# A transformer layer with two kinds of attention: the causal part's order, later features, and the last norm's root on ScalarE

## The chip, the cores and the metric

The kernel runs on one core of a Trainium2 chip. The metric is the device time of one execution in microseconds (us), the median of several runs; lower is better. Times within the kernel come from a profile of one execution. The engines are TensorE (PE, with its weight loads PEld), VectorE (DVE), ScalarE (ACT), GpSimd (POOL) and SyncE (SP), which here only issues DMAs.

## What is computed

A layer in three parts, each with a layer norm before and a residual after. All numbers are float32. `x` is 4 x 256 x 256 (batch, token, channel), the context 4 x 4096 x 256, with 16 heads of 16 channels.

```python
x = x + cross_attention(layernorm(x), ctx, ctx)     # softmax over 4096 context rows
x = x + causal_attention(layernorm(x))              # positive features, no softmax
x = x + ffn(layernorm(x))                           # silu(x Wg) * (x Wu), then Wd; hidden 768

# causal_attention, for each batch and head:
qf, kf = features(q), features(k)   # exp(clip(omega . x/|x| * sqrt(2 s) - s)), 64 features
ctx[t] = sum_{u <= t} (qf[t] . kf[u]) v[u]
den[t] = max(sum_{u <= t} qf[t] . kf[u], 1e-6)
out = (ctx / den) @ Wout + bout
```

## The kernel before

The first 1063 us are the cross attention; the change touches what follows, the **causal part** and the feed-forward part that is woven into it (lines 374 to 594 of the kernel).

Work is cut by batch `b` (4, of 256 tokens, two row tiles of 128) and by quad `q` (4 heads). A step `n` from 0 to 15 is one quad of one batch, `n = 4 b + q`. `attend(n)` (line 413) makes three functions of a step.

- `scores` (420): on TensorE the products of key and query features, into four PSUM banks `pa` (lines 427 and 432). Two of them are copied to `at` by ScalarE (438) and masked by GpSimd (439); the other two are masked by VectorE on the way out (444).
- `values` (447): `at` times V, the sums of four heads in one bank `po` (453); ScalarE copies it to `avT` (458). V has a column of ones, so the denominators come along.
- `divide` (461), once for two quads: transposes `avT` into `pt_o` on TensorE (465), then three VectorE instructions: the clamp and reciprocal of `den` (470, 471) and the product into `att` (472).

`features(n)` (273) makes the features of quads `n` and `n + 1` in one go: eight products into four banks `pf` (281), four clips on VectorE (287), four exponentials on ScalarE (288), four factors on GpSimd (289). Those of the first six quads are made during the cross attention.

`output(b)` (479) transposes `att` of a batch (`tr_o`, 486), copies it on ScalarE (`oT`, 487), multiplies by Wout (`py`, 492) and adds to the residual stream `xr` (493). `feed_forward(b)` (495) makes four functions: `norm` (layer norm, on VectorE), `turn` (transposes `tr_z`, 509, copied to `zT` by ScalarE, 510), `hidden(m)` for three pairs of 128 columns (`pg` and `pu`, 518; tanh on ScalarE, 522; two VectorE instructions into `hT`, 523 and 524) and `down(i)` for the two row tiles (`pd`, twelve products in all, 530; the sum, 534; the store, 535).

There are two layer norms in the code. `layernorm` (96) takes the root with ScalarE's Sqrt (109) and a reciprocal on VectorE. `normalised` (137), used in this part, finds the inverse root on VectorE alone with `inverse_root` (120): two instructions for a first guess and three for each of three refinements.

What sets the order: TensorE, ScalarE, VectorE and SyncE run their instructions in the order in which the program writes them (`manual_schedule`, line 539); GpSimd's order is left to the framework. A loop over `n` from 0 to 16 (584) writes, for each step, the values of the step before, the scores of this one, the divide when `n` is even, a features call for the steps in `early`, and then what the list `fills[n]` holds. All PSUM tiles come from one pool of eight banks.

The `fills` hold the pieces of other work. `weight(n)` (402) turns a piece of the integer feed-forward weights, which `weight_load` (395) brings by DMA on SyncE's queue, into floats on ScalarE, and starts the load after next. `normalise`, `turn15` and `project15` (819, 845, 853) end the cross attention: `normalise` transposes the last sums (`pt_x`), divides them on VectorE (`rd`, `on`), adds a bias on GpSimd (836) and sends them with eight DMAs on SyncE's queue into rows (`xo`, 840); `turn15` transposes those rows (`px`, 849) and `project15` multiplies them by Wh (`py` at line 159) and adds to `xr` (858). Until then the norm of the last batch (`norm3`) can't start, nor its `turn3` (`tr`, 208, copied to `zT` by VectorE, 209), its queries and keys (`qk3`, products `pqk`, sum at 221) and values (`v3`). `normed`, `qk_normed` (259) and `qk_turned` (264, 265) turn them into the input of features 12 and 14.

For batch `b`, output and norm stand in step `4b + 4`, the turn in the step behind it, hidden and down in the steps from there on. For the last batch everything is in step 16, with what is left of the batch before it.

Of the kernel before, what the change touches and what calls it, by code (L numbers as in the profile page):

```python
# [12 lines left out]
F32 = mybir.dt.float32  # L13
I32 = mybir.dt.int32
AF = mybir.ActivationFunctionType
# [5 lines left out]
P = 128  # L21
B, T, D = 4, 256, 256
# [12 lines left out]
NH = HID // P  # L35
# [4 lines left out]
def perceiver_layer(  # L40
# [5 lines left out]
    nc = tc.nc  # L46
# [17 lines left out]
    eps = const.tile([P, 1], F32, tag="eps", name="eps")  # L64
# [31 lines left out]
    def layernorm(z, tiles):  # L96

        n = len(tiles)
        mv = lnp.tile([P, n, 2], F32, tag="ln_mv", name="ln_mv")
        rs = lnp.tile([P, n], F32, tag="ln_rs", name="ln_rs")  # L100

        def stats():
            for i, t in enumerate(tiles):
                st = lnp.tile([P, 6], F32, tag="ln_st", name="ln_st")
                nc.vector.bn_stats(st, xr[:, t, :])
                nc.vector.bn_aggr(mv[:, i, :], st)

        def root():
            nc.scalar.activation(rs, mv[:, :, 1], AF.Sqrt, bias=eps)

        def scaled():
            nc.vector.reciprocal(rs, rs)
            for i, t in enumerate(tiles):
                nc.vector.tensor_scalar(
                    z(t), xr[:, t, :], mv[:, i, 0:1], rs[:, i : i + 1], ALU.subtract, ALU.mult
                )

        return stats, root, scaled
# [18 lines left out]
    def normalised(z, tiles):  # L137

        n = len(tiles)
        mv = lnp.tile([P, n, 2], F32, tag="ln_mv", name="ln_mv")  # L140
        for i, t in enumerate(tiles):
            st = lnp.tile([P, 6], F32, tag="ln_st", name="ln_st")
            nc.vector.bn_stats(st, xr[:, t, :])
            nc.vector.bn_aggr(mv[:, i, :], st)
        v = lnp.tile([P, n], F32, tag="ln_v", name="ln_v")
        nc.vector.tensor_scalar(v, mv[:, :, 1], LN_EPS, None, ALU.add)
        rs, pieces = inverse_root(v)
        for piece in pieces:
            piece()
        for i, t in enumerate(tiles):  # L150
            nc.vector.tensor_scalar(
                z(t), xr[:, t, :], mv[:, i, 0:1], rs[:, i : i + 1], ALU.subtract, ALU.mult
            )
# [31 lines left out]
    def bank(shape, name):  # L185

        return psum.tile(shape, F32, tag="b", name=name)
# [187 lines left out]
    late = ctx.enter_context(tc.tile_pool(name="late", bufs=1))  # L375
# [4 lines left out]
    for i in (0, 2):  # L380
# [2 lines left out]
            pattern=[[1, P]], channel_multiplier=-1,  # L383
        )
    att = late.tile([P, NT, D], F32, tag="att", name="att")

# [13 lines left out]
    def weight(n):  # L402
        i, half = divmod(n, 2)
        w = ws[i].shape[1] // 2
        nc.scalar.activation(
            ws[i][:, half * w : half * w + w, :], coming.pop(n), AF.Copy, scale=(1.0, 0.5, 1.0)[i] / 127.0
        )
        if n + 2 < 6:
            weight_load(n + 2)
# [69 lines left out]
    def output(b):  # L479
        tiles = (2 * b, 2 * b + 1)  # L480
        oTs = []
        for t in tiles:
            oT = work.tile([P, KC, P], F32, tag="oT", name="oT")
            ps = bank([P, KC, P], "tr_o")
            for k in range(KC):
                nc.tensor.transpose(ps[:, k, :], att[:, t, k * P : (k + 1) * P], ident)
            nc.scalar.copy(oT, ps)
            oTs.append(oT)
        for t, oT in zip(tiles, oTs):
            py = bank([P, D], "py")  # L490
            for k in range(KC):
                nc.tensor.matmul(py, lhsT=oT[:, k, :], rhs=wout_sb[:, k, :], start=k == 0, stop=k == KC - 1)  # L492
            nc.vector.tensor_tensor(xr[:, t, :], py, xr[:, t, :], ALU.add)

    def feed_forward(b):

        tiles = (2 * b, 2 * b + 1)
        z = work.tile([P, 2, D], F32, tag="z", name="z")
        zT = work.tile([P, KC, T], F32, tag="zT", name="zT")
        hT = work.tile([P, NH, T], F32, tag="hT", name="hT")  # L500

        def norm():
            normalised(lambda t: z[:, t % 2, :], tiles)

        def turn():
            ps = bank([P, KC, 2, P], "tr_z")
            for j in range(2):
                for k in range(KC):
                    nc.tensor.transpose(ps[:, k, j, :], z[:, j, k * P : (k + 1) * P], ident)
            nc.scalar.copy(zT.rearrange("p k (j t) -> p k j t", t=P), ps)  # L510

        def hidden(m):
            pg, pu = bank([P, 2, T], "pg"), bank([P, 2, T], "pu")
            for ps, w in ((pg, wg), (pu, wu)):
                for i in range(2):
                    ns = slice((2 * m + i) * P, (2 * m + i + 1) * P)
                    for k in range(KC):
                        nc.tensor.matmul(  # L518
                            ps[:, i, :], lhsT=w[:, k, ns], rhs=zT[:, k, :], start=k == 0, stop=k == KC - 1
                        )  # L520
            th = work.tile([P, 2, T], F32, tag="th", name="th")
            nc.scalar.activation(th, pg, AF.Tanh, scale=0.5)
            nc.vector.scalar_tensor_tensor(th, th, 1.0, pg, ALU.add, ALU.mult)
            nc.vector.tensor_tensor(hT[:, 2 * m : 2 * m + 2, :], pu, th, ALU.mult)

        def down(i):
            t = tiles[i]
            pd = bank([P, D], "pd")
            for n in range(NH):
                nc.tensor.matmul(  # L530
                    pd, lhsT=hT[:, n, i * P : (i + 1) * P], rhs=wd[:, n, :], start=n == 0, stop=n == NH - 1
                )
            o = work.tile([P, D], F32, tag="o", name="o")
            nc.vector.tensor_tensor(o, pd, xr[:, t, :], ALU.add)
            nc.sync.dma_start(out=out[t * P : (t + 1) * P, :], in_=o)

        return norm, turn, hidden, down

    with tc.manual_schedule(engines={ET.PE, ET.Activation, ET.DVE, ET.SP}):
        normalise, turn15, project15 = finish  # L540
        normalise()
        for n in range(2):
            weight_load(n)
        NB = B * NQ
        fills = {n: [] for n in range(NB + 1)}
        norm3, turn3, qk3, sq3, v3, _ = causal_in(3)
        for n in range(6):
            fills[n + 1] += [lambda n=n: weight(n)]
        fills[2] += [turn15]
        fills[3] += [project15, norm3]  # L550
        fills[4] += [turn3, lambda: qk3(0)]
        fills[5] += [lambda: qk3(1), lambda: sq3(0), v3, lambda: sq3(1), lambda: normed((6, 7))]
        fills[6] += [lambda: qk_normed(6), lambda: qk_normed(7)]
        fills[7] += [lambda: qk_turned(6), lambda: qk_turned(7)]
        ff = {}

        def call(b, part, *args):
            return lambda: ff[b][part](*args)

        def begin(b):  # L560
            ff[b] = feed_forward(b)
            ff[b][0]()

        for b in range(B):
            n0 = 4 * b + 4
            turn, down = call(b, 1), [call(b, 3, i) for i in range(2)]
            hidden = [call(b, 2, m) for m in range(NH // 2)]
            fills[n0] += [lambda b=b: output(b), lambda b=b: begin(b)]
            if b < B - 1:
                fills[n0 + 1] += [turn]  # L570
                fills[n0 + 2] += [hidden[0]]
            if b < B - 2:
                fills[n0 + 3] += [hidden[1]]
                fills[n0 + 4] += [hidden[2]]
                fills[n0 + 5] += down
            elif b == B - 2:
                fills[n0 + 3] += [hidden[1]]
                ends = [hidden[2]] + down
            else:
                fills[n0][:0] = ends[:1]  # L580
                fills[n0] += ends[1:] + [turn] + hidden + down
        early = {0: 6, 2: 8, 4: 10, 8: 12, 10: 14}
        steps = [attend(n) for n in range(NB)]
        for n in range(NB + 1):
            if n > 0:
                steps[n - 1][1]()
            if n < NB:
                steps[n][0]()
            if n > 0 and n % 2 == 0:
                steps[n - 1][2]()  # L590
            if n in early:
                features(early[n])
            for piece in fills[n]:
                piece()
# [503 lines left out]
```

## Time and profile before

| | us |
|---|---|
| median of 3 runs | 1214.21 (1213.54 to 1215.38) |
| the profiled execution | 1214.88 |
| its span in the profile | 1213.2 |
| end of the cross attention's last products | 1063.1 |
| PE busy | 1183.5 (98%) |
| DVE busy | 905.8 (75%) |
| ACT busy | 686.8 (57%) |
| POOL busy | 142.3 (12%) |
| mean granted TensorE clock | 0.999 |

The busy time is a share of the whole span. The change can act on the last 150 us alone, so the readings below are of stretches of it. In rows of the timeline the columns are: start and length in us, engine, line, operation, output and inputs, shapes, count of instructions; in brackets the idle time of the engine before the row and who ended it. A row merges instructions of one kind, and its count of matmuls is a multiple of the program's products, since one product of floats is several matmuls.

### The profile page before, as it was taken

The page shows a single profiled execution, that of the slowest core. Times are in us where ns is not written, and L with a number is a line of the kernel's source. Part 1 is how long each engine was busy: PE and PEld are TensorE (multiplying, and loading weights), DVE is VectorE, ACT ScalarE, POOL GpSimd, SP SyncE. Part 2 cuts the span into 40 slices and gives each one's busy share as a digit, 9 for nine tenths or more (in the row PEclk, how much of TensorE's full clock was granted, in tenths as well). Part 3 has the DMA queues.
Part 4 walks back from the last instruction along what each step waited for, and adds up shares of the span by engine and source line. Part 5 has one row for each costly group of instructions (what it writes and reads, how often), then busy time and mean ns, then how long its engine had stood idle before and what let it go on. Part 6 is the DMA issues. An engine that isn't in the chain of part 4 may idle for free.

```text
span 1213.2 us, 42834 instructions
## 1 busy us (share of the span) xinstructions
PE 1183.5 (98%) x17970; PEld 799.5 (66%) x17970; DVE 905.8 (75%) x1751; ACT 686.8 (57%) x1429; POOL 142.3 (12%) x282
## 2 busy tenths in 40 slices
PE   7999999999999999999999999999999999969998
PEld 3566667666766676667766776677667655546777
DVE  6887777777777777777777777777788887577653
ACT  3346665666656666666566655666666546853421
POOL 4010101010101010101010101010101113131210
PEclk9999999999999999999999999999999999999999
DMA  6452342233223322332223222332233000020000
GB/s 210 135 178 63 106 117 73 62 106 120 73 59 104 99 83 71 90 105 92 73 86 106 95 74 81 96 99 68 79 105 101 22 2 4 2 69 14 10 9 18
DMA packets 62032, 95.90 MB, mean 79 GB/s; under 512 B 32912, under 2 KB 35600, under 8 KB 61840
## 3 DMA queue, kind: packets, MB, share of 16 engines
q1 hardware_dynamic: 57072, 92.44, 25.3%
q8 instruction: 142, 2.33, 0.8%
q0 software_dynamic: 4352, 0.07, 0.3%
q10 hardware_dynamic: 416, 0.66, 0.2%
q14 instruction: 50, 0.41, 0.1%
HBM read 74.17 MB, written 1.05 MB: 62 GB/s over the span
## 4 chain that ended last, share of the span: by engine, by line
PE 91%; DVE 5%; ACT 1%; DMA 1%; issue 1%; POOL 0%; DVEq 0%; ACTq 0%
PE pt L779 22%; PE pm L732 18%; PE pav L799 18%; PE pv L159 11%; PE pk L159 10%; PE pd L530 2%; PE pg L518 2%; PE pu L518 1%; PE pq L880 1%; PE pqk L159 1%; DVE mx L739 1%; PE pa L427 1%; PE py L492 1%; DVE kt L287 1%; PE py L159 1%
## 5 line engine op out<-in xcount | busy, mean ns | idle before, releaser
L739 DVE TENSOR_REDUCE mx<-pm 128x1 f32<-128x512 f32 x1024 | 635.6, 684 | 145.9 <-PE pm L732 145.7
L784 ACT ACTIVATE e<-pt 128x512 f32<-128x512 f32 x1024 | 529.2, 603 | 375.0 <-PE pm L732 351.1
L779 PE MATMUL pt<-qa,kt 32*128 32x256 f32 x4096 | 499.8, 388 | 2.5 <-DMA qa<-neg 1.2
L732 PE MATMUL pm<-kt,qT 32*128 32x512 f32 x2048 | 495.0, 616 | 0.1
L779 PEld LDWEIGHTS pt<-qa,kt 32*128 32x128 f32 x4096 | 316.9, 184 | 122.9 <-ACT v L703 43.2
L799 PE MATMUL pav<-e,v 128*32 128x256 f32 x4096 | 269.6, 379 | 0.0
L732 PEld LDWEIGHTS pm<-kt,qT 32*128 32x128 f32 x2048 | 172.3, 184 | 16.6 <-issue 3.9
L799 PEld LDWEIGHTS pav<-e,v 128*32 128x32 f32 x4096 | 129.7, 110 | 72.4 <-issue 3.9
L809 DVE TENSOR_TENSOR av<-pav,av 128x256 f32<-128x256 f32 x240 | 101.7, 424 | 65.4 <-PE pav L799 65.1
L159 PE MATMUL pv<-wv_sb,ctx 128*32 128x128 f32 x4096 | 137.5, 276 | 0.0
L159 PE MATMUL pk<-ctx,wk_sb 128*32 128x256 f32 x2048 | 136.9, 389 | 0.0
L159 PEld LDWEIGHTS pv<-wv_sb,ctx 128*32 128x32 f32 x4096 | 104.3, 109 | 43.5 <-DVE mx L739 42.4
L755 POOL DMA_DIRECT2D qa<-neg x120 | 64.0, 541 | 559.8 <-issue 559.8
L159 PEld LDWEIGHTS pk<-ctx,wk_sb 128*32 128x32 f32 x2048 | 54.8, 110 | 66.8 <-DVE mx L739 39.4
L675 ACT ACTIVATE ku<-pk,bk_sb 128x256 f32<-128x256 f32 x128 | 63.3, 496 | 12.5 <-PE pk L159 9.6
L703 ACT COPY v<-pv 128x256 f32<-128x256 f32 x128 | 51.8, 405 | 9.9 <-PE pv L159 9.9
L836 POOL TENSOR_TENSOR on<-on,bv_sb 128x64 f32<-128x64 f32 x32 | 9.1, 304 | 191.9 <-DVE on L831 150.2
L288 ACT ACTIVATE kt<-kt,shift 128x512 f32<-128x512 f32 x32 | 22.4, 725 | 12.4 <-DVE kt L287 12.4
L444 DVE TENSOR_TENSOR at<-pa,mask 128x384 f32<-128x384 f32 x32 | 16.3, 551 | 13.9 <-PE pa L432 13.8
L287 DVE TENSOR_SCALAR kt<-pf,low,top 128x512 f32<-128x512 f32 x32 | 23.7, 803 | 2.8 <-PE pf L281 2.6
L518 PE MATMUL pg<-zT,wg 128*128 128x256 f32 x96 | 23.3, 386 | 0.7 <-ACT zT L510 0.7
L518 PE MATMUL pu<-zT,wu 128*128 128x256 f32 x96 | 22.7, 379 | 0.0
(131 smaller groups left out, 576.4 us busy)
## 6 DMA issues: line engine op xcount, KB each, us to landing
ctx<-in_ctxT_dram SPq DMA_DIRECT2D x128, 512.0 KB
kt<-ku SPq DMA_DIRECT2D x508, 32.0 KB
xo<-on SPq DMA_DIRECT2D x128, 8.0 KB
qa<-neg POOLq DMA_DIRECT2D x120, 0.5 KB, 2.4
xr<-in_x_dram SPq DMA_DIRECT2D x4, 256.0 KB
out_dram<-o SPq DMA_DIRECT2D x8, 128.0 KB
wqkv_sb<-in_wqkv_dram SPq DMA_DIRECT2D x1, 768.0 KB
w_i<-in_w_gate_dram SPq DMA_DIRECT2D x2, 384.0 KB
```

The lines of the kernel that those rows point to most:

```text
L159: nc.tensor.matmul(out[js], lhsT=lhsT[:, js], rhs=rhs, **flags)
L287: nc.vector.tensor_scalar(f, pf.rearrange("p s t -> p (s t)"), low, top, ALU.max, ALU.min)
L518: nc.tensor.matmul(ps[:, i, :], lhsT=w[:, k, ns], rhs=zT[:, k, :], start=k == 0, stop=k == KC - 1)
L675: nc.scalar.activation(ku[:, cs], made.pop(), AF.Identity, bias=bk_sb[:, m : m + 1])
L703: nc.scalar.copy(to.rearrange("p t (h d) -> p t h d", d=HD + 1)[:, :, :, :HD], made.pop().rearrange("p t (h d) -> p t h d", d=HD),)
L732: nc.tensor.matmul(pm, lhsT=qT[rows, q, t0 : t0 + P], rhs=kt[rows, c * CH : (c + 1) * CH], start=True, stop=True,)
L739: nc.vector.tensor_reduce(mx[:, i, j, c : c + 1], pm, AX.X, ALU.max)
L755: nc.gpsimd.dma_start(out=qa[32 * j : 32 * j + 1, i * P : (i + 1) * P], in_=neg[:, j, i : i + 1])
L779: nc.tensor.matmul(pt[:, i, :], lhsT=kt[rows, ks], rhs=qa[rows, :], start=True, stop=True)
L784: nc.scalar.activation(e, pt, AF.Exp, scale=0.25)
L799: nc.tensor.matmul(pav[32 * h : 32 * h + 32, :], lhsT=v[:, t % KT, c0 : c0 + 32], rhs=es[n, h][:, i, :], start=i == 0, stop=i == 1,)
L809: nc.vector.tensor_tensor(avs[u], pav, avs[u], ALU.add)
```

## The change

Four things are done.

1. **Order within a step.** The scores of step `n` are written ahead of the values of step `n - 1`. The divide leaves the loop and goes into the `fills`: at steps 4, 8, 12 and 16 directly ahead of `output` (at step 4 behind `turn3` and `qk3(0)`, at steps 8 and 12 behind a `hidden` of the batch before), at steps 2, 6, 10 and 14 as the second piece.
2. **Features later.** Those of quads 8, 10, 12 and 14 move from steps 2, 4, 8 and 10 to steps 6, 8, 10 and 12; those of quad 6 stay in step 0.
3. **`normalise` later.** It moves from ahead of the loop into step 0, behind the first scores and features; the first two weight loads so come ahead of its DMAs on SyncE's queue.
4. **The tail.** The norm of the last batch is `layernorm`, with its root on ScalarE. A Sqrt of one column stands ahead of it behind the last `output`, and a Tanh behind it; each writes a tile `spare` that no one reads. The second `down` of batch 2 is cut in two halves of three products, with the last batch's `turn` between them.

```diff
+    spare = late.tile([P, 1], F32, tag="spare", name="spare")
...
         def norm():
-            normalised(lambda t: z[:, t % 2, :], tiles)
+            if b < B - 1:
+                normalised(lambda t: z[:, t % 2, :], tiles)
+            else:
+                for piece in layernorm(lambda t: z[:, t % 2, :], tiles):
+                    piece()
+                nc.scalar.activation(spare, eps, AF.Tanh)
...
-        def down(i):
+        pds = {}
+
+        def down(i, parts=range(NH)):
             t = tiles[i]
-            pd = bank([P, D], "pd")
-            for n in range(NH):
+            if i not in pds:
+                pds[i] = bank([P, D], "pd")
+            pd = pds[i]
+            for n in parts:
                 nc.tensor.matmul(
                     pd, lhsT=hT[:, n, i * P : (i + 1) * P], rhs=wd[:, n, :], start=n == 0, stop=n == NH - 1
                 )
+            if NH - 1 not in parts:
+                return
...
-        normalise()
         for n in range(2):
             weight_load(n)
...
+        fills[0] += [normalise]
         fills[2] += [turn15]
         fills[3] += [project15, norm3]
         fills[4] += [turn3, lambda: qk3(0)]
...
-            fills[n0] += [lambda b=b: output(b), lambda b=b: begin(b)]
+            fills[n0] += [lambda n=n0: steps[n - 1][2](), lambda b=b: output(b)]
+            if b == B - 1:
+                fills[n0] += [lambda: nc.scalar.activation(spare, eps, AF.Sqrt)]
+            fills[n0] += [lambda b=b: begin(b)]
...
             else:
-                fills[n0][:0] = ends[:1]
-                fills[n0] += ends[1:] + [turn] + hidden + down
-        early = {0: 6, 2: 8, 4: 10, 8: 12, 10: 14}
+                fills[n0][1:1] = ends[:1]
+                split = [call(B - 2, 3, 1, parts) for parts in (range(3), range(3, NH))]
+                fills[n0] += ends[1:2] + split[:1] + [turn] + split[1:] + hidden + down
+            fills[n0 - 2][1:1] = [lambda n=n0 - 2: steps[n - 1][2]()]
+        early = {0: 6, 6: 8, 8: 10, 10: 12, 12: 14}
         steps = [attend(n) for n in range(NB)]
         for n in range(NB + 1):
+            if n < NB:
+                steps[n][0]()
             if n > 0:
                 steps[n - 1][1]()
-            if n < NB:
-                steps[n][0]()
-            if n > 0 and n % 2 == 0:
-                steps[n - 1][2]()
             if n in early:
                 features(early[n])
             for piece in fills[n]:
                 piece()
```

Here `n0 = 4 b + 4`, `call(b, part, ...)` calls a function of batch `b`'s feed-forward part, and `begin(b)` makes that part and runs its norm.

## The prediction

> **What bounds it.** First the page: its slices and its chain.
>
> ```profile
> PE   7999999999999999999999999999999999969998
> ...
> PE 91%; DVE 5%; ACT 1%; DMA 1%; issue 1%; POOL 0%; DVEq 0%; ACTq 0%
> ```
>
> TensorE sets the time; its one hole is the 6, the slice from 1061.6 to 1091.9, where the causal part begins (1063). So I read the busy time in windows of 10 us there.
>
> ```profile
> 1070.00:1080.00 10.00, 7.28 (x86) 4.92 (x86) 5.33 (x11) 5.32 (x11) 3.27 (x8) 1.00 0.41 122
> 1080.00:1090.00 10.00, 6.05 (x72) 3.85 (x72) 9.15 (x31) 5.64 (x12) 4.21 (x9) 1.00 0.28 80
> 1090.00:1100.00 10.00, 8.04 (x60) 4.10 (x60) 4.60 (x13) 3.88 (x8) 2.71 (x5) 0.83 0.13 39
> ...
> 1130.00:1140.00 10.00, 10.00 (x86) 8.25 (x86) 5.82 (x22) 2.68 (x6) 1.57 (x4) 1.00 0.08 28
> ```
>
> First PE, PEld, DVE, ACT, POOL busy, then clock. Up to 1095 TensorE waits; from 1098 on it is full. A gain can come from the head alone, and whatever makes TensorE wait after 1098 is a loss. Third, the timeline of the head:
>
> ```profile
> 1065.57 5.28 SPq L840 DMA_DIRECT2D xo<-on  x8
> ...
> 1071.59 1.23 PE L453 MATMUL po<-at,va 128*32 128x256 f32 x16 [2.40 <-POOL at L439]
> ...
> 1077.05 0.44 PE L849 MATMUL px<-ident,xo 128*128 128x128 f32 x2
> ...
> 1091.72 3.43 PE L159 MATMUL pqk<-wqkv_sb,zT 128*32 128x512 f32 x16 [3.97 <-DVE zT L209]
> ```
>
> TensorE's gaps there (0.52, 2.40, 0.91, 0.71, 1.20, 3.97, 0.24) are 9.95 us; the pqk behind the longest took 1.5 us more than the next pqk (1.93 at 1100.20), at half clock. So 11.5 us can be won at most. The eight copies of on to xo were issued long before px (1077.05) reads them.
>
> Fourth, a step with features behind it (step 8):
>
> ```profile
> 1120.82 1.15 PE L281 MATMUL pf<-qT,om_sb 32*128 32x256 f32 x16
> ...
> 1122.11 2.96 DVE L287 TENSOR_SCALAR kt<-pf,low,top 128x512 f32<-128x512 f32 x4
> ...
> 1125.72 0.58 ACT L522 ACTIVATE th<-pg 128x512 f32<-128x512 f32 x1
> ...
> 1126.62 1.99 PE L492 MATMUL py<-wout_sb,oT 128*128 128x256 f32 x8 [0.56 <-ACT oT L487]
> 1127.13 0.69 DVE L524 TENSOR_TENSOR hT<-pu,th 128x512 f32<-128x512 f32 x1
> ```
>
> The tanh stands behind four exponentials (1122.94 to 1125.82), so hT ends (1127.82) 2.4 us after pu (1125.46). Nobody waits: att was divided earlier (1121.28 to 1122.1), and tr_o runs at once, at 1125.46.
>
> **The change, part by part** (times below as us after 1000).
>
> *The head, steps 0 to 4.* Removed from it: 2 of 3 feature groups (8 and 10), so 2 x 1.08 of TensorE, 2 x 2.95 of VectorE, 2 x 2.88 of ScalarE. Moved: normalise behind scores(0) and features(6), two weight loads ahead of its eight DMAs on SP's queue (0.8 us of issue, waiting only for the last pav, so free). I lay the old durations in the new order. pa(0) 63.15, 1.50 long; pf to 65.73; pt_x to 66.17. VectorE: masks 64.76 to 65.78, four clips to 68.73, and only then rd and on, to 69.3 (before: 65.1). GpSimd adds the bias at 69.4 or, behind the last factor, 70.1. The first xo issue was 0.33 after that add, the last landing 6.5 after the first issue (landing event at 72.09). So xo lands at 76.25 to 76.95; I take 76.6. TensorE: pa(1) to 67.67, po(0) to 68.46, pa(2) to 70.4 (banks), po(1) from 71.1 (its select) to 72.3, pt_o(1) to 73.1 (avT(1), behind weight(0) and at(2) on ScalarE). Then px waits: **a new gap of 3.5 us**; queued behind it is all of TensorE. px 76.65, pa(3), po(2), py to 80.42; xr and norm3, 4.80 us from the row before (81.63 to 86.43), to 85.29. TensorE has pa(4) and po(3) until 82.7, then waits for z (2.2), and for zT (1.3, behind the masks of step 4). pqk 86.94 to 88.75; pt_o(3) to 89.19, then 1.2 us for att, as the divide now stands directly ahead of output(0). tr_o 90.4, py 91.3 to 93.3. Before, py ended at 98.0: 4.7 earlier, but with 2.16 of pf still owed: **-2.5**. Landing alone puts +-0.35 on it.
>
> *Clock.* Rows: after a 2.40 us gap no slowing, after 3.97 us half clock and 1.5 us lost. The new gap of 3.2 to 3.9 lies between, so 0 to 1.5; as its middle is about as near to one as to the other in what they cost, I take half, **+0.8**.
>
> [...]
>
> *Steps 5 to 7.* VectorE must do after output(0) what it did before (norm 4.98, masks, L221 to L255; 12.8 us to the end of at(6)) and then 2.95 of clips. Banks go round a ring of eight: this row waits for the bank that hT frees, though others are free:
>
> ```profile
> 1114.29 1.59 PEld L518 LDWEIGHTS pg<-zT,wg 128*128 128x128 f32 x8 [0.29 <-DVE hT L524]
> ```
>
> In the new order pg(0) takes the bank of pa(6)'s third product, read by VectorE at 12.35 after py, while TensorE is there at 10.0; tr_qk and the next pg wait about 0.8 more for hT. hidden(1) ends 22.85 after py; before 20.0 (98.0 to 118.0) plus the 1.08 paid here: **+1.8**, between 0.6 (any free bank) and 2.4.
>
> *Steps 8 and 12.* The divide now follows hidden(2) in program order, so on VectorE it is behind hT. From scores: pa and po 2.30, clips 0.83 after pf begins, hT 5.71 after the first clip (1122.11 to 1127.82), divide 0.9 (1121.28 to 1122.1), tr_o, oT 0.95, py 1.99: 12.7. TensorE is through pt_o at 7.3 and **waits 2.4 us for att**; tr_o, py and all later steps are queued behind that wait. Before, step 8 took 10.6 (1118.01 to 1128.61): **+2.1**. Step 12 took 9.02 (1150.27 to 1159.29), plus the 1.08 of the pf that lands here: **+2.6**. A divide behind hidden at 10 and 14 delays no one: its att is read two steps later.
>
> *Masked products a step earlier* after 1098: the selects and masks were in time there (no gap), worth 0.
>
> *Tail.* Tanh and Sqrt tables: one load each, 1.28 us by the page's load row (ACT), between oT (1185.76) and the statistics (1189.07), and behind the root: ScalarE had idled 7.42 there. Eleven small VectorE steps become one root (0.30) and a reciprocal, so z ends near 1190.5 instead of 1192.2; half of the last pd (1.3 us) covers zT, and this gap goes:
>
> ```profile
> 1193.82 2.00 PE L518 MATMUL pg<-zT,wg 128*128 128x256 f32 x8 [0.67 <-ACT zT L510]
> ```
>
> **-0.7**. Without that cover it is 0; with both loads on the path +2.6.
>
> **Sum**: -2.5 + 0.8 + 1.8 + 2.1 + 2.6 - 0.7 = +4.1 us. The profiled execution took 1214.88 (span 1213.2 and 1.7 around it), 0.67 over the median of 1214.21; I put the sum on the median: **1218.3 us**.
>
> **Rivals.**
> 1. *Not slower: att is there in time at 8 and 12.* If hT ended before pt_o (tanh not behind the exponentials), 4.7 goes: 1213.6. For it: pg ends (1123.9) 1.8 us before the tanh begins. Against: ScalarE's order is fixed, and row 1125.72 shows the delay. It decides if hT ends before 7.3 after scores instead of 8.8. 0.12.
> 2. *The head is cheaper: px doesn't wait for xo.* Landing by 73.1 takes off 3.5 and the clock's 0.8: 1214.0; if all 11.5 us of the head went, 9.0 more than I count: 1209.3. For it: GpSimd doesn't keep program order (a select of step 4 ran at 1085.47, ahead of step 3's L200 at 1086.26). Against: on comes behind the clips on VectorE. 0.20.
> 3. *Half clock at both waits* (px, then z and zT, 3.5 of 4.2 us idle): the other 0.7 and 1.5 more: 1220.5. For it: the second idle stretch has 0.65 us of tr in 4.2. Against: at 1067.5 to 1070.9 half an idle window passed unslowed. 0.11.
> 4. *The table loads fall on the path*: -0.7 becomes +2.6: 1221.6. For it: Sqrt stands ahead of the root on ScalarE. Against: 3.3 us are free there for 1.28. 0.02.
>
> My forecast has 0.55, its own range 1216.2 to 1219.6 (landing 0.35, banks -1.2 to +0.6, clock 0.7 to either side, not all at once). With the rivals: 1212.0 to 1221.0, leaving out rival 2's far end and rival 4. 0.2% is 2.4 us, about what a measurement of this kernel tells from none. Faster: half of rival 2 and some of 1, 0.15. Same (1211.8 to 1216.6): the rest of both and the forecast's edge, 0.23. Slower: 0.62.
>
> **What would show it.** px beginning at 1076 to 1077, after 3 to 4 us of idle; the clock in the slice behind it; TensorE idle some 2.4 us ahead of tr_o at steps 8 and 12, released by att; pg(0) at step 6 waiting for an at of VectorE; zT covered and no gap ahead of the last pg. I am wrong if tr_o runs on at 8 and 12, or if xo lands before pt_o(1) ends.

## The result and the profile after

The changed kernel takes **1223.62 us** (median of 4 runs, 1223.27 to 1223.95), the kernel before 1214.26 beside it (4 runs, 1213.54 to 1215.38): a ratio of 1.0074 [1.0062, 1.0086], 9.4 us slower. The forecast was 1218.3 and its range ended at 1221.0. So the sign was right, and the size was outside the range. One execution of the kernels below, the profiled one of e5, took 2229.8 us at a granted clock of 0.88, and its trace is not read (without it the median of e5 is 1210.86).

The profiled execution took 1223.48 us, its span is 1221.6. From the page of the kernel after, the slices of TensorE, its granted clock, and the chain that ended last:

```profile
PE   7999999999999999999999999999999999978998
...
PEclk9999999999999999999999999999999999989999
...
PE 92%; DVE 5%; ACT 1%; DMA 1%; issue 0%; SPq 0%; POOL 0%; ACTq 0%; DVEq 0%
```

The slice that read 6 before reads 7 here (it is 1068.9 to 1099.4), the next one reads 8 instead of 9, and the chain is as it was. Read alone, the 7 looks like a fuller head. But the 8 in the clock stands in the same slice, where before had 9 throughout: a part of that busy time is the same work at half speed.

The steps were placed by their distance from the last pav, the cross attention's last product (it ends at 1062.04 here, at 1063.12 before). First the timeline of the head, kernel after:

```profile
1068.54 5.31 SPq L855 DMA_DIRECT2D xo<-on  x8
...
1075.58 0.66 PE L864 MATMUL px<-ident,xo 128*128 128x128 f32 x2 [3.80 <-DMA xo<-on]
1076.17 1.23 PE L428 MATMUL pa<-kt 64*128 64x256 f32 x4
...
1086.39 0.67 PE L208 MATMUL tr<-ident,z 128*128 128x128 f32 x4 [2.56 <-DVE z L151]
...
1088.24 3.22 PE L159 MATMUL pqk<-wqkv_sb,zT 128*32 128x512 f32 x16 [1.18 <-DVE zT L209]
```

The eight copies of on now go out at 1068.5 instead of 1065.6, and px waits 3.80 us for the last of them. The row of pa behind it shows what I did not look for far enough: 1.23 us for four instructions that take 0.70 at full clock (the row at 1081.46, granted clock 1.00). TensorE comes back from the wait at half speed, and is so again for the pqk behind the waits for z and zT (granted clock 0.50 in both places, in the windows below).

Step 8 of the kernel after, from the same view:

```profile
1125.65 0.58 ACT L528 ACTIVATE th<-pg 128x512 f32<-128x512 f32 x1
...
1127.05 0.69 DVE L530 TENSOR_TENSOR hT<-pu,th 128x512 f32<-128x512 f32 x1
...
1128.14 0.42 DVE L473 TENSOR_TENSOR att<-pt_o,den 128x256 f32<-128x256 f32 x1
...
1128.62 0.90 PE L487 MATMUL tr_o<-ident,att 128*128 128x128 f32 x3 [2.43 <-DVE att L473]
1129.56 3.12 PE L493 MATMUL py<-wout_sb,oT 128*128 128x256 f32 x8
```

The tanh stands where it stood, behind the exponentials. Its hT is about as late as before, but the divide (L471 to L473) is now behind it on VectorE, and tr_o waits 2.43 us for att. That is the wait that was forecast (2.4). Then py takes 3.12 instead of 1.99. Step 12 repeats it, and there the products of pa behind py are slow too:

```profile
1164.19 0.55 PE L487 MATMUL tr_o<-ident,att 128*128 128x128 f32 x3 [2.43 <-DVE att L473]
1164.98 2.82 PE L493 MATMUL py<-wout_sb,oT 128*128 128x256 f32 x8 [0.24 <-ACT oT L488]
1167.73 1.22 PE L428 MATMUL pa<-kt 64*128 64x256 f32 x4
```

The same stretches by windows, kernel after: stretch and its length, then busy PE, PEld, DVE, ACT, POOL with the number of instructions, granted clock, DMA share, GB/s. The windows are cut where the clock changes in this trace:

```profile
1070.43:1073.85 3.42, 1.23 (x14) 0.52 (x7) 1.00 (x4) 1.59 (x4) 0.79 (x2) 1.00 0.14 12
1073.85:1077.26 3.41, 1.68 (x8) 1.21 (x10) 0.42 (x1) 0.00 (x0) 0.00 (x0) 0.50 0.70 222
1077.26:1080.67 3.41, 3.41 (x34) 2.36 (x34) 1.02 (x2) 0.93 (x3) 0.79 (x2) 0.50 0.04 14
...
1084.09:1087.50 3.41, 0.67 (x4) 0.40 (x4) 3.10 (x14) 0.92 (x2) 1.17 (x2) 1.00 0.41 123
1087.50:1090.91 3.41, 2.67 (x16) 0.68 (x16) 0.60 (x1) 0.00 (x0) 0.34 (x1) 0.50 0.02 8
1125.05:1128.46 3.41, 1.14 (x8) 0.80 (x6) 2.03 (x5) 1.17 (x2) 0.96 (x2) 1.00 0.01 2
1128.46:1131.87 3.41, 3.21 (x9) 2.35 (x10) 0.31 (x2) 0.74 (x2) 0.00 (x0) 0.50 0.00 0
1162.59:1166.00 3.41, 1.57 (x8) 1.23 (x9) 1.45 (x4) 0.65 (x2) 0.00 (x0) 1.00 0.00 0
1166.00:1169.42 3.42, 3.42 (x15) 2.41 (x15) 1.91 (x7) 0.00 (x0) 0.00 (x0) 0.50 0.00 0
```

Read them in pairs. A window in which TensorE was busy 1.23, 0.67, 1.14 or 1.57 us is followed by one at clock 0.50 (behind the first by two; in the window at 1073.85 TensorE was busy for 1.68 of 3.41 us). None of these windows is idle, and at steps 8 and 12 the gap in them is 2.43 us. Half clock stands for 17.1 us of the causal part (before: 3.4, from 1091.40 on, behind a window without any work of TensorE), and TensorE works through 14.4 us of it. At half speed that is about 7.2 us lost, an estimate, where before lost about 1.5.

The last row shown of before, the pg that waited 0.67 us for zT in the tail, has no gap here:

```profile
1202.40 1.89 PE L524 MATMUL pg<-zT,wg 128*128 128x256 f32 x8
```

### The profile page after: what moved, and what is told of

Its sections match the earlier page's. It is cut to its first block, busy times and chain, and to the rows that moved or that the text cites. A ratio compares the mean times of both kernels' runs of the same rounds, so it can differ in the third digit from the quotient of the medians.

```text
span 1221.6 us, 42842 instructions
## 1 busy us (share of the span) xinstructions
PE 1189.2 (97%) x17970; PEld 802.7 (66%) x17970; DVE 904.1 (74%) x1740; ACT 690.3 (57%) x1434; POOL 143.3 (12%) x282
## 4 chain that ended last, share of the span: by engine, by line
PE 92%; DVE 5%; ACT 1%; DMA 1%; issue 0%; SPq 0%; POOL 0%; ACTq 0%; DVEq 0%
PE pt L794 22%; PE pm L747 18%; PE pav L814 18%; PE pv L159 11%; PE pk L159 10%; PE pd L540 2%; PE pg L524 1%; PE pq L895 1%; PE pu L524 1%; PE pa L428 1%; PE pqk L159 1%; DVE mx L754 1%; PE py L493 1%; PE po L454 1%; PE pf L281 1%; PE py L159 1%
## 5 line engine op out<-in xcount | busy, mean ns | idle before, releaser
L439 ACT COPY at<-pa 128x384 f32<-128x384 f32 x32 | 13.7, 482 | 27.7 <-PE pa L433 25.6
L428 PE MATMUL pa<-kt 64*128 64x256 f32 x128 | 23.5, 432 | 0.0
```

Source lines behind the costliest of these rows:

```text
L428: nc.tensor.matmul(pa[:, 0:2, :], lhsT=kf[rows, :P], rhs=qf[rows, :], start=True, stop=True)
```

## The experiments

Two theories were set against each other first. **W**: the new waits of TensorE (px, z, att at 8 and 12), at the lengths that the sum gave them, make the difference, and the clock adds little. **C**: behind each of these waits the clock is halved, and the halved windows cost as much again or more; W + C is the sum of both. A third, **Q**, came with e2: what hurts in the head is the order of SyncE's queue, in which weight loads and the eight copies stand behind one another. Times are medians, and ratios are to the kernel before, run in the same batch on the same chip (1214.77, 1214.59 and 1214.99 in the three batches).

| kernel | us | ratio to before |
|---|---|---|
| e1: after, divide first at 4, 8, 12 | 1215.85 | 1.0009 [1.0000, 1.0019] |
| e2: after, normalise first | 1225.96 | 1.0096 [1.0080, 1.0111] |
| e3: e1 and e2 | 1216.76 | 1.0019 [1.0010, 1.0029] |
| e4: after, products in the waits | 1217.59 | 1.0023 [1.0012, 1.0033] |
| e5: e1, normalise behind the first loads | 1211.00 | 0.9966 [0.9954, 0.9979] |
| e6: before, tail of the change | 1214.19 | 0.9998 [0.9988, 1.0007] |
| e7: before, scores ahead of values | 1219.59 | 1.0041 [1.0026, 1.0056] |
| e8: before, later features | 1215.74 | 1.0006 [0.9996, 1.0016] |
| e9: before, loads ahead of normalise | 1214.24 | 0.9993 [0.9983, 1.0002] |
| e10: e5 again | 1210.47 | 0.9963 [0.9950, 0.9976] |
| e11: e10, values ahead of scores | 1213.02 | 0.9980 [0.9971, 0.9990] |
| e12: e10, products in the waits for z and zT | 1208.28 | 0.9947 [0.9932, 0.9962] |

### The clock by itself: e4

The kernel after, with products into a bank that the next product of the program overwrites: eight ahead of px, five ahead of the last batch's tr, five ahead of tr_o at steps 8 and 12. They fill the waits and take none away; what is computed stays the same.

```diff
+                for _ in range(8 if u == NU - 1 else 0):
+                    nc.tensor.matmul(
+                        px.rearrange("p k c -> p (k c)"), lhsT=ident, rhs=rest[8][:, 0, :], start=True, stop=True
+                    )
...
+            for _ in range(5 if b in (1, 2) and t == tiles[0] else 0):
+                nc.tensor.matmul(
+                    ps.rearrange("p k c -> p (k c)"), lhsT=ident, rhs=wout_sb[:, 0, :], start=True, stop=True
+                )
```

> The changed kernel, order and waits untouched, with products whose result is overwritten put into four of its gaps: eight (some 3.4 us) ahead of px, five (some 2.1 us) ahead of tr of the last batch and of tr_o at steps 8 and 12. They fit in the gaps, so they delay nothing, but TensorE is busy there. Theory W+C: the waits stay, the half clock goes (17 us of it in the causal part, about 7 us of time on the products that ran in it): 1216.5 to 1218.5. Rival W (waits alone): no change, 1223 to 1224.5. Rival B (it is not idleness that halves the clock): the half clock stays in the record, 1223 to 1225.

It took 1217.59, 6.0 us less than the kernel after. The timeline of e4 at step 8:

```profile
1123.67 2.32 PE L491 MATMUL tr_o<-wout_sb,ident 128*128 128x256 f32 x10
...
1126.37 0.55 PE L495 MATMUL tr_o<-ident,att 128*128 128x128 f32 x3 [0.27 <-DVE att L477]
1127.17 1.99 PE L501 MATMUL py<-wout_sb,oT 128*128 128x256 f32 x8 [0.24 <-ACT oT L496]
```

Its windows in the head:

```profile
1073.85:1077.26 3.41, 2.99 (x15) 2.28 (x13) 0.25 (x1) 0.00 (x0) 0.00 (x0) 1.00 0.36 56
1077.26:1080.67 3.41, 3.41 (x52) 2.36 (x52) 1.47 (x4) 1.75 (x4) 0.79 (x2) 1.00 0.46 184
```

att still comes when it comes (the first row's ten instructions are the five added products), px still begins 13.6 us after the last pav, and yet py is back at 1.99 and the clock is 1.00 in every stretch of the causal part that was read. The result lies in the range of W + C and outside those of its rivals. What remains over before, 2.8 us by the medians of this batch, is the waits and the moved work without the clock. C is worth 6.0 by the medians of the two kernels (6.5 if each is set against the before of its own batch, 9.36 less 2.82). From the end of the pu before it to the end of its py, step 8 takes 12.79 us here and step 12 takes 12.78, against 14.05 and 13.6 in the kernel after.

### The divide at steps 8 and 12: e1

```diff
-            fills[n0] += [lambda n=n0: steps[n - 1][2](), lambda b=b: output(b)]
+            if b < B - 1:
+                fills[n0][:0] = [lambda n=n0: steps[n - 1][2]()]
+                fills[n0] += [lambda b=b: output(b)]
+            else:
+                fills[n0] += [lambda n=n0: steps[n - 1][2](), lambda b=b: output(b)]
```

> The changed kernel, with the divides of steps 4, 8 and 12 written first in their step's list instead of directly ahead of output. Theory W+C (waits for att, and the half clock that each wait sets off): the two gaps of 2.43 us ahead of tr_o shrink to the 0.56 that step 8 had before the change, the gap of 0.94 at step 4 goes, and the half clock after 1128 and 1166 goes (3.1 and 3.4 us of products at half speed, so 1.55 and 1.7): 3.7 + 0.9 + 3.2, about 8 less than 1223.6: 1215.5 to 1217. Rival W (waits alone, the half clock costs nothing that ends up in the time): 4.6 less, 1219. Rival N (TensorE would be late at these places anyhow, by VectorE's queue): 1222 to 1224.

1215.85, 7.8 us less than the kernel after, by one moved piece, and within the range of W + C alone. The timeline of e1 at step 8:

```profile
1126.09 0.42 DVE L473 TENSOR_TENSOR att<-pt_o,den 128x256 f32<-128x256 f32 x1
1126.35 0.58 ACT L528 ACTIVATE th<-pg 128x512 f32<-128x512 f32 x1
1126.58 0.60 PE L487 MATMUL tr_o<-ident,att 128*128 128x128 f32 x4
...
1127.42 1.99 PE L493 MATMUL py<-wout_sb,oT 128*128 128x256 f32 x8 [0.24 <-ACT oT L488]
...
1127.75 0.69 DVE L530 TENSOR_TENSOR hT<-pu,th 128x512 f32<-128x512 f32 x1
```

VectorE now makes att ahead of hT: it ends at 1126.51, just after the tanh has begun, tr_o runs on, and hT's lateness is nobody's again. The waits of 2.43 are gone at both steps and their halved windows with them; px still waits 3.78 us and the head has 13.7 us of half clock (10.2 in the kernel after). output(0)'s py ends 34.0 us after the last pav, against 33.8, so moving the divide at step 4 gained nothing in all: the gain lies at steps 8 and 12 and in the products right behind them.

### Normalise: e2, e3, e5, e10, e9

e2 puts `normalise()` back ahead of the weight loads; e3 does that and e1's edit.

```diff
+        normalise()
         for n in range(2):
             weight_load(n)
...
-        fills[0] += [normalise]
```

> The changed kernel, with normalise back ahead of the loop and of the weight loads. Theory W+C: xo lands some 3 us earlier than px needs it, so the gap of 3.80 ahead of px goes, and the half clock from 1073.8 to 1080.7 (2.5 us on 5.1 us of products); part comes back because z and zT of the last batch are still waited for: 4 to 6 less, 1217.5 to 1219.5. Rival W: 3 to 3.8 less, 1220 to 1220.5. Rival H (the head is bound by the norm's chain on VectorE, px or not): 1 less or nothing, 1222.5 to 1224.

> Both edits of the two runs before it together: divides of steps 4, 8, 12 first in their lists, normalise ahead of the loop. Theory W+C: the two gains add, 8 + 5: 1209.5 to 1212, which is below the kernel before (1214.3), since the later features then take two feature groups out of the head and the tail gains 0.7. Rival W: 1214.5 to 1216.

Both missed: 1225.96 and 1216.76, no gain at all over their partners without this edit (1223.62 for the kernel after, 1215.85 for e1). The timeline of e2, with SyncE's queue (SPq), ScalarE and TensorE:

```profile
1070.56 0.82 SPq L401 DMA_DIRECT2D w_i<-in_w_gate_dram  x2
1074.57 0.84 ACT L406 ACTIVATE wg<-w_i 128x768 f32<-128x768 int32 x1 [3.81 <-DMA w_i<-in_w_gate_dram]
...
1076.48 0.69 PE L466 MATMUL pt_o<-ident,avT 128*128 128x128 f32 x2 [4.18 <-ACT avT L459]
```

px waits no longer, but the weight load is now issued behind the eight copies (1070.56). ScalarE, which converts the weight (L406) ahead of the next avT in its order, waits 3.81 us for it, and pt_o behind avT waits 4.18. One wait was exchanged for another of the same length. So the loads have to be first and normalise early: e5 puts `normalise()` between the loads and the loop, with e1's divide.

```diff
         for n in range(2):
             weight_load(n)
+        normalise()
...
-        fills[0] += [normalise]
```

> The kernel with the divides first (1215.85), and normalise ahead of the loop but behind the two weight loads. Theory Q (in the run with normalise ahead of both, ScalarE's weight conversion waited 3.8 us for the load that had gone behind the eight xo copies on SP's queue, and avT, pt_o and px behind it): now neither copy is late, the gap ahead of px goes and the half clock with it: 3.8 + 2.5 less, and perhaps 1 of it given back at z: 1209 to 1212. Rival H (the head is bound by VectorE's chain through the last batch's norm): 1214 to 1216.

> The kernel with the divides first and normalise behind the two loads, ahead of the loop, once more, for its trace. Theory W+C: 1211 within 1; no gap ahead of px or pt_o(1), at z and zT of the last batch gaps of some 1.6 and 1.9 us as in the kernel with the divides alone, no half clock before them, perhaps one window of 3.4 us behind them. Rival H: a gap of the same sum stands at z and zT instead of px.

1211.00 and, run again, 1210.47: faster than before in both batches, by 3.6 and 4.5 us. The timeline of e10:

```profile
1072.95 0.41 PE L868 MATMUL px<-ident,xo 128*128 128x128 f32 x2
...
1081.38 0.72 PE L208 MATMUL tr<-ident,z 128*128 128x128 f32 x4 [1.63 <-DVE z L151]
...
1083.96 1.08 PE L159 MATMUL pqk<-wqkv_sb,zT 128*32 128x512 f32 x4 [1.86 <-DVE zT L209]
```

px has no wait, and the head is left with z and zT, behind which 4.9 us of TensorE's work is still done at half clock, in two windows where one at most was expected. Whether the order of the queue also helps the old kernel is asked by e9: `normalise()` behind the loads, in the kernel before.

> The kernel before, with the two first weight loads ahead of normalise's eight copies on SP's queue, nothing else. Theory Q: ScalarE's wait of 3.0 us for the load goes, at and avT of steps 1 and 2 come sooner, the gap of 0.91 ahead of pt_o goes; the 3.97 for zT, set by VectorE's clips, stays: 0.5 to 1.5 less than before. Rival (VectorE alone sets the head): no change.

1214.24 against 1214.99: not told from nothing, and its causal part has one halved window more (from 1073.0) than before's. So Q holds for the new schedule: e3 and e5 differ in nothing but this order, and e5 is 5.8 us faster. In the old one ScalarE's wait for the load (3.01 us in before) goes as well, but the waits of po (2.40) and of zT (3.97) stay, and the order of the queue is worth too little to see.

### The parts of the change alone: e6, e7, e8, e11

e6 is before with the tail's edits (layernorm, Sqrt, Tanh, the split `down`); e7 with the scores ahead of the values, and nothing else; e8 with the later features.

```diff
+            if n < NB:
+                steps[n][0]()
             if n > 0:
                 steps[n - 1][1]()
-            if n < NB:
-                steps[n][0]()
```

```diff
-        early = {0: 6, 2: 8, 4: 10, 8: 12, 10: 14}
+        early = {0: 6, 6: 8, 8: 10, 10: 12, 12: 14}
```

> The kernel before, with the tail's edits alone: the last norm's root on ScalarE, the two table loads, and the last down in halves around the turn. Theory: the gap of 0.67 ahead of the last batch's pg is covered and z is ready in time: 0.7 less than before. Rival (the table loads reach the path): 1 to 2.6 more than before.

> The kernel before, with the scores of a step ahead of the last step's values, all else as it was (divide in the loop, early features, normalise first). Theory: the waits of po for the selects in the head (2.40 and 1.20) shrink, up to 3.6 less; after the head nothing changes, since the selects were in time there: 1211 to 1214. Rival (the waits move to z and zT, which VectorE sets behind the clips): within 1 of before, at either side.

> The kernel before, with the features of quads 8, 10, 12, 14 made at steps 6, 8, 10, 12 and all else as it was. Theory: two groups of clips, exponentials and factors leave the head, the wait of 3.97 for zT shrinks below 2 and the half clock of 1091 goes; 2.2 of products come back later and steps 6 and 7 lose up to 1.8 by banks: 2 to 4 less than before, 1210.5 to 1213. Rival (the later steps lose more than the head gains, by waits at 6 to 12): 1215 to 1218.

e6: 1214.19, 0.4 under before, which the runs can't tell from nothing; in its trace the gap of 0.67 is gone and the stretch from the last pav to the last pd is 145.6 us instead of 146.5. e7: 1219.59, 5.0 slower, which neither theory gave. Its timeline shows e2's wait again, since `normalise()` stands ahead of the loads in before:

```profile
1074.47 0.84 ACT L405 ACTIVATE wg<-w_i 128x768 f32<-128x768 int32 x1 [4.17 <-DMA w_i<-in_w_gate_dram]
...
1076.38 0.69 PE L465 MATMUL pt_o<-ident,avT 128*128 128x128 f32 x2 [4.54 <-ACT avT L458]
```

The short waits of before (2.40 us and less) are mostly merged into one of 4.54, the wait for zT grows from 3.97 to 4.79, and behind each of the two the clock is one half for 6.83 us. e8: 1215.74, not told from no change, and within the range of its rival. The wait of 3.97 for zT becomes 1.77 for z and 1.92 for zT, so the head ends earlier, and steps 6 to 12 give it back (tr_qk waits 0.49 and 1.38, py 0.56 at steps 8 and 12, and the features are paid there).

e11 asks what the order is worth once the head is mended: e10 with the values ahead of the scores.

> The kernel of e10 with the values of the last step ahead of the scores again, as in the kernel before. If the order of scores and values earns something once nothing else is late in the head: the waits of po for the selects come back in the head, 0.5 to 3 more than e10. Rival (the order moves waits but adds none): within 0.7 of e10.

1213.02, 2.5 us more than e10: the wait of 2.40 ahead of po returns, with halved windows at 1071.9 and 1085.6. The same edit that costs 5.0 us in the old schedule earns 2.5 in the mended one. The two schedules differ in more than the queue's order, so that this order alone turns the sign is argued from the waits and not shown.

### Both cures: e12

e10 with three added products ahead of the last batch's tr and four ahead of its first pqk, overwritten as in e4.

```diff
+            for _ in range(3 if b == B - 1 else 0):
+                nc.tensor.matmul(
+                    ps[:, 0].rearrange("p i c -> p (i c)"), lhsT=ident, rhs=rest[8][:, 0, :], start=True, stop=True
+                )
...
+            for _ in range(4 if b == B - 1 and i == 0 else 0):
+                nc.tensor.matmul(ps[:, :D], lhsT=ident, rhs=rest[8][:, 0, :], start=True, stop=True)
```

> The kernel of e10 with products whose result is overwritten in its two gaps: three (1.3 us) ahead of tr of the last batch, four (1.7 us) ahead of its first pqk. Theory W+C: if e10 has a window at half clock behind these gaps, it goes, 1 to 1.7 less than e10; if it has none, no change or up to 0.5 more. Rival W: no change in either case.

1208.28, 2.2 us less than e10 (1 to 1.7 were expected) and 6.7 less than before, the best of all. Three of its four executions took 1208.1 to 1208.3 at a granted clock of 0.999; the fourth took 1210.32 at 0.997, so the cure did not always hold. The timeline of e12:

```profile
1079.58 1.46 PE L207 MATMUL tr<-wout_sb,ident 128*128 128x256 f32 x6
1081.28 0.77 PE L212 MATMUL tr<-ident,z 128*128 128x128 f32 x4 [0.24 <-DVE z L151]
1081.88 1.89 PE L221 MATMUL pqk<-wout_sb,ident 128*128 128x256 f32 x8
1083.96 0.64 PE L159 MATMUL pqk<-wqkv_sb,zT 128*32 128x512 f32 x4 [0.18 <-DVE zT L213]
```

pqk begins at the same 1083.96 as in e10; what is saved is its pace (0.64 us for the four instructions that took 1.08) and that of what follows.

## Why the prediction was right or wrong

**The step that failed is the term "Clock, +0.8".** It measures 6.0 (the kernel after against e4), and takes up nearly all of the 5.3 us by which the forecast fell short. The prediction said: "after a 2.40 us gap no slowing, after 3.97 us half clock", and so gave half of 1.5 to the new gap of 3.5 us and nothing to the others. Two things in that are wrong. The gap of 2.40 in before lay in a window (1067.50 to 1070.91) in which TensorE was still busy for 1.69 of 3.41 us, and it was not a length that is always spared: the two gaps of 2.43 were not. Four stretches, not one, were followed by half clock: px, z with zT, and att at steps 8 and 12. By the traces, the head cost 3.6 us of it (output(0)'s py ends 33.8 us after the last pav; 30.2 in e4), step 8 cost 1.3, and step 12 cost 0.8 up to the end of its py and 0.8 in the products behind it. That is 6.5, against 6.0 or 6.5 by the medians. Rival 3, half clock at both waits of the head, came true in its place: its price for the head, 3.0, measures 3.6. The 2.9 us of steps 8 and 12 had no rival.

**The other terms were right in size, some of them by luck.** Without the clock the sum was +3.3, to 1217.5; e4, the same kernel kept at full clock, took 1217.59 (+2.8 on its own before). Term by term, predicted against measured:

- *Head*: px at +13.5 us after the last pav, measured +13.5, with a gap of 3.80 for 3.5. Two small errors cancel in it: the first copy went out 0.1 to 0.8 us sooner than computed, and px began 7.0 us behind it instead of 6.5. output(0)'s py at +30.2: 30.2 in e4.
- *Steps 5 to 7*: hidden(1) ends 22.85 after that py; 22.74 in e4. The size came out, the place did not: pg(0), which was to wait for the at of VectorE, runs on (1106.01), and the pu behind it waits 0.17 for that at. The longer waits are tr_qk's, 0.53 for its input kt and 0.55 behind VectorE's work on hidden(0) (L529). That they add up to the forecast is luck.
- *Steps 8 and 12*: 12.7 each; 12.79 and 12.78 in e4. A gap of 2.4; 2.43, twice. Rival 1 (att in time) fell.
- *Tail*: the gap of 0.67 is gone and neither table load is on the path, so rival 4 fell; from output(3)'s py to the last pd it is 21.2 us instead of 22.1, and by the median of e6 the gain is 0.4, not told from nothing.
- *Rival 2*, a head without px's wait, fell for the kernel as changed. It came true in e10, by another way than the one given for it: normalise early, but the loads earlier still.
- *Masked products ahead, worth 0*: as part of the sum it did no harm. By itself the order is worth −2.5 or +5.0 us (e11, e7), by what stands on ScalarE ahead of avT. The prediction credited normalise's move with an issue that was "free" on SyncE's queue, and missed that the queue's order would decide the place of the wait: this is what e2 and e7 showed in their timelines.

The parts run alone (e6, e7, e8: −0.4, +5.0, +1.2) do not add up to the whole (+9.4). They leave out the new places of the divide and of normalise, and a part is not worth the same in another schedule: e7 and e11 show this for the order of scores and values.

## What to carry to other kernels

Where TensorE sets the time, price a wait by what the trace shows behind it, and by how empty it leaves the window around it (3.41 us long here), not by its length alone: four waits of 2.4 to 3.8 us here cost 6.0 us on top of themselves, and overwritten products in them gave it back. Before an instruction is moved behind another on an in-order engine, ask who is late there without harm (hT at steps 8 and 12): its lateness becomes that of all that is put behind it. A small copy that is moved up a queue can push a load that another engine needs at once (ScalarE waited 3.81 us for it in e2), so move the pair together and keep the load first.

## What the runs showed of the hardware

**The clock changed on a grid of 3.413 us, and the window ahead of a halved one need not be idle.** In the records of the kernels before and after the clock changes only at multiples of 3.413 us from one another (the 12 times at which a clock begins in the record of the kernel after agree within 2 ns modulo that length). Against the kernel the grid lies in another place in each: half clock begins at 1091.40 before and at 1073.85 after, 5.14 lengths apart. In the other profiles the edges are estimates, worked out from the granted clock of the stretches read (e1: 0.59 from 1073.85 to 1077.26, so half clock from 1074.46) and from the pace of TensorE's rows; the busy shares are so good to about 2 points.

So the windows between the last pav and the last pd were counted in 12 profiles: before, after, e1, e2, e4 and e6 to e12. Of those that began at full clock, all 17 in which TensorE was busy for 44% or less were followed by half clock (the emptiest with 0% in before, the fullest with 44% in e11). Between 45 and 52% it went either way: 46% in after and 52% in e10 were followed by half clock, 45% in e8, 48% in e6 and 50% in before (the window that misled me) were not, so the busy share alone does not settle it there. None with 55% or more was followed by half clock. At half clock, windows that were busy 73 and 77% (e2) were followed by another at half, one of 78% (after, from 1087.50) by full clock. That the busy share is more than a companion is what e4 and e12 show: with products added to the waits, e4 has a granted clock of 1.00 in the windows in which the kernel after has 0.50, and e12 has 1.00 from 1080.67 to 1090.91, where e10 has 0.67, 0.50 and 0.83.

Left open: in the kernel after, one halved window stands in the cross attention, near 1022.6 (granted clock 0.51 from 1022.58 to 1026.00). The window ahead of it, from 1019.17 to 1022.58, has 2.69 us of TensorE's work in 3.41, well above the shares at which windows of the causal part were halved, and no run here says why it was halved. In e4 and e12 the mean granted clock is 0.999, though no stretch read of their causal part shows half clock: by it 1 to 4 us of half clock, an estimate, stand elsewhere in each, and where was not shown.
